# The opening attentions of a fused two-layer block: a third group's normalisation passes moved to ScalarE, a fourth group's statistics moved to other turns

## The chip, the core and the metric

The kernel runs on one core of a Trainium2 chip. The metric is device time in microseconds (us); the kernel before takes 888.03 us, the median of three runs (887.79 to 888.46). A difference of about 0.2% (1.8 us) is what a measurement of this kernel can tell from no change.

A core has engines that run their own instruction lists side by side and wait for one another by semaphores: TensorE (PE in the profile, its weight loads PEld), VectorE (DVE), ScalarE (ACT), GpSimd (POOL) and SyncE (SP, which here only issues DMA transfers).

## The reference, cut to what matters

The input x holds 64 sequences of 32 rows of 256 numbers. Six steps add to it in turn; each starts from a layer norm of x:

```
x = x + window cross attention(norm(x), ctx)   # 16 heads of 16, rotary
x = x + causal self attention(norm(x))         # 16 heads of 16, rotary
x = x + linear in fp8(norm(x))
x = x + cross attention over 257 keys(norm(x), ctx)
x = x + gated mixer(norm(x))
x = x + mixture of 8 experts, top 2, plus a shared one(norm(x))
```

The norm is `y = (x - mean) / sqrt(variance + 1e-5)` over the 256 numbers of a row. The change touches only the first step, and of it the norm of the third and fourth quarter of the rows.

## The kernel before, in words

The 2048 rows are four groups (g = 0 to 3) of 512 rows, a group being four tiles of 128 rows. `small_attentions` (L250) computes the first two steps as eight units of work, n = 0 to 7: layer one's groups 0 to 3, then layer two's. Before its loop it prepares units 0 and 1. The loop then goes over n, and in each n over four turns t = 0 to 3; a turn is written (n, t) here. In turn (n, t) the scores of tile t of unit n are computed, older tiles are carried on by one step each (turned, context, by_feature, project), and unit n+1 is prepared: `rotated` makes one half of its keys (t = 0, 1) or queries (t = 2, 3), `values` its values (even t), `spread_keys` spreads its keys by head.

Unit n+2 is prepared earlier still. `norm_steps` (L115) is a generator that gives its norm in four pieces: the statistics (four bn_stats on DVE), the aggregation with a start value for the inverse root (four bn_aggr and three small instructions on DVE) and three Newton steps on POOL (twelve small instructions on 128x4, called the root chain here), then the normalised rows y, two tiles at a time (one pass on DVE each, or, with `by_act`, one ACTIVATE on ACT with a scale and an offset; the offset takes two more small instructions on POOL). `prepare(count)` takes so many pieces. Which turn takes how many is written by hand in three tables of four numbers, `ahead` (before `rotated`), `behind` (after `by_feature`) and `at_end` (after the sums). `opened` transposes y on PE (eight transposes into two psT tiles) and ACT copies the two psT tiles to yT, from which the queries are made.

The order on each engine is as the code issues it, without a scheduler (`in_order`). All engines run their lists strictly in order, so an instruction that waits holds back what stands behind it. DMA issues stand in SP's list: the four swapped blocks of a rotation (far<-part), the values' way through memory (v_rows<-v, then vb<-v_rows in `blocks`), and loads of later weights and of x.

PSUM tiles of `rotated` (ps_qk), `values` (ps_v) and `opened` (psT) take three banks in turn (b0, b1, b2, in `pa`). So the second psT of turn (1, 0) needs the bank in which ps_qk of the same turn stands until ACT has read it (near<-ps_qk).

Of the kernel before, what the change touches and what calls it, by code (L numbers as in the profile page):

```python
# [20 lines left out]
NG, NT = 4, 4  # L21
# [44 lines left out]
def perceiver_kernel(ctx: ExitStack, tc: tile.TileContext, a: dict, out: bass.AP):  # L66
# [121 lines left out]
    def finish(pieces):  # L188

        while True:  # L190
            try:
                next(pieces)
            except StopIteration as end:
                return end.value

    def ring(pool, *tags):

        count = [0]

        def get(shape, name, dt=F32):  # L200
            tag = tags[count[0] % len(tags)]
            count[0] += 1
            return pool.tile(shape, dt, tag=tag, name=name, bufs=1)

        return get
# [13 lines left out]
    def transposed(y, bank, yT):  # L219

        for pair in range(y.shape[1] // 2):
            ps = bank([P, 2, 2 * P], "psT")
            for c in range(2):
                for i in range(2):
                    turn(
                        ps[:, c, i * P : (i + 1) * P],
                        y[:, 2 * pair + i, c * P : (c + 1) * P],
                        ident,
                    )
            scalar.copy(yT[:, :, pair * 2 * P : (pair + 1) * 2 * P], ps)  # L230
        return yT
# [18 lines left out]
    def small_attentions(layers, first_loads, decode, sides, load_layer1, layer1):  # L250
# [33 lines left out]
        def fetch(n):  # L284
            layer, g = order[n]
            if not layer["from_ctx"]:
                return None
            kvT = kvTs([P, 2, GT], "kvT")
            sync.dma_start(out=kvT, in_=a["ctx32T"][g])
            return kvT  # L290
# [6 lines left out]
        def group(n, kvT):  # L297

            layer, g = order[n]
            return dict(layer, n=n, g=g, kvT=kvT)  # L300

        def opened(it):
            yT = transposed(it["y"], pa, yTs([P, 2, GT], "yT"))
            it["yT"] = yT
            if not it["from_ctx"]:
                it["kvT"] = yT
# [78 lines left out]
        def blocks(it, half):  # L385
            vb = vbs[it["n"] % 2]
            it["vb"] = vb
            rows_h = v_rows[it["i"], it["g"]][half * D : (half + 1) * D].rearrange(
                "(b k) d -> k b d", k=S
            )  # L390
            for h in range(4):
                sync.dma_start(
                    out=vb[half][S * h : S * (h + 1), :, h].rearrange("k b g e -> k b (g e)"),
                    in_=rows_h[:, :, 64 * h : 64 * (h + 1)],
                )
# [108 lines left out]
        order = [(layer, g) for layer in layers for g in range(NG)]  # L504
# [15 lines left out]
        after = group(1, fetch(1))  # L520
# [6 lines left out]
        adds = [rotated(it, 1, c) for c in range(2)]  # L527
# [21 lines left out]
        now = it  # L549

        line = [None] * 5
        adds, early_y = [], None
        layer1_loads = load_layer1()
        for n in range(len(order) + 1):
            if n > 0:
                after = coming
            if after is not None:
                after["kb"] = [None, None]
            kvT = coming = None
            if n + 2 <= last:  # L560
                side = norm_steps(order[n + 2][1], apart=True)
            else:
                side = sides

            def prepare(count):
                y = None
                for _ in range(count if n + 2 <= last else 0):
                    try:
                        next(side)
                    except StopIteration as end:  # L570
                        y = end.value
                return y

            ahead, behind, at_end = (
                ((0, 1, 0, 1), (1, 0, 1, 0), (0, 0, 0, 0))
                if n
                else ((0, 0, 0, 0), (0, 0, 1, 0), (0, 1, 0, 2))
            )

            for t in range(NT):  # L580
                if (n, t) == (last + 1, 2):
                    shared_bank[0] = ring(psum, "b0", "b1")
                    late_bank.append(ring(psum, "b7", "b5"))
                if line[2]:
                    turned(line[2])
                kb_now = None
                if n <= last:
                    if t < 2:
                        kb_now = (now, 1, t)
                    elif after is not None:  # L590
                        kb_now = (after, 0, t - 2)
                due, adds = adds, []
                if t == 0 or n == 0:
                    for add in due:
                        add()
                    due = []
                    if n == last:
                        add_bias(n - 2, NT - 1)
                if kb_now:
                    spread_keys(*kb_now, 0)  # L600
                if line[4] and (n, t) != (last - 1, NT - 1):
                    project(line[4])
                if after is None:
                    next(layer1, None)
                else:
                    y = prepare(ahead[t])
                    adds.append(rotated(after, *((1, 0), (1, 1), (0, 0), (0, 1))[t]))
                    if (n, t) == (0, 0):
                        blocks(now, 0)
                    elif (n, t) == (0, 1):  # L610
                        opened(after)
                    elif (n, t) == (0, 3):
                        next(loads)
                    if (n, t) == (last - 1, NT - 1):
                        project(line[4])
                        sums(line[2])
                if line[3]:
                    by_feature(line[3])
                prepare(behind[t])
                if n + 2 > last:  # L620
                    next(side, None)
                    if n > last:
                        next(side, None)
                if n > 0 and (n, t) != (last - 1, NT - 1):
                    add_bias(n - 1, t)
                if n > 0 and (n, t) != (1, 0) and (t % 2 == 0 or n + 2 > last):
                    next(decode, None)
                for add in due:
                    add()
                if kb_now:  # L630
                    spread_keys(*kb_now, 1)
                if after is None:
                    next(layer1, None)
                elif t % 2 == 0:
                    values(after, t // 2)
                    if (n, t) == (0, 2):
                        blocks(now, 1)
                    elif (n, t) == (1, 0):
                        after["y"] = early_y
                        opened(after)  # L640
                elif t == 3:
                    for half in range(2 if n < last - 1 else 1):
                        blocks(after, half)
                    if n + 2 <= last:
                        coming = group(n + 2, kvT)
                        if n > 0:
                            coming["y"] = y
                            opened(coming)
                line[0] = scores(now, t) if n <= last else None
                if (n, t) == (last, NT - 1):  # L650
                    pair_pool.close()
                    later_psum.append(
                        attention.enter_context(tc.tile_pool(name="at_late", bufs=1, space=PSUM))
                    )
                if line[2]:
                    context(line[2])
                if (n, t) == (last - 1, NT - 1):
                    next(layer1)
                    blocks(after, 1)
                if line[1] and (n, t) != (last - 1, NT - 2):  # L660
                    sums(line[1])
                if last >= n > last - 2:
                    next(side, None)
                early_y = prepare(at_end[t])
                if t == (0 if n else 1) and n <= last - 2:
                    kvT = fetch(n + 2)
                elif n < 3 and (n, t) not in ((0, 0), (0, 2)):
                    next(loads, None)
                elif n >= last - 2:
                    next(layer1_loads, None)  # L670
                line = [None] + line[:-1]
            now = after
# [1548 lines left out]
```

## Time and profile before

| what | us |
|---|---|
| median of 3 runs | 888.03 |
| the profiled execution | 888.15 |
| its span, first to last instruction | 886.4 |
| what lies around the span | 1.75 |
| PE busy | 851.0 (96% of the span) |
| DVE, POOL, ACT busy | 576.1, 513.9, 438.5 |
| mean granted clock of TensorE | 0.992 |

Times within the kernel are us from the start of the span. A line of the timeline gives start, duration, engine, line (L107 and L119 are helpers that record nearly every operation), operation, output<-input with shapes, the number of instructions joined, and in square brackets how long the engine was idle before and what ended that idle time. The turns concerned begin with the transposes of probabilities on PE (ps_t<-cst,e): (1, 0) at 41.63, (1, 1) at 51.07, (1, 2) at 55.73, (1, 3) at 63.30, (2, 0) at 68.83 and (2, 1) at 75.22.

### The profile page before, as it was taken

What the parts mean: (1) busy time and instruction counts of PE and PEld (TensorE: products, weight loads), DVE (VectorE), ACT (ScalarE), POOL (GpSimd) and SP (SyncE); (2) the same over time, 40 slices, a digit from 0 to 9 for tenths busy, and PEclk for the clock granted to TensorE, in tenths of its full rate; (3) what the DMA queues carried; (4) which work ended last, traced back from release to release, by engine and by line L of the source; (5) the groups of instructions that cost most, each with busy time, mean ns of one, the idle gap of its engine ahead of it and who ended that gap; (6) DMA issues with size and microseconds to landing.
All of it is one profiled execution on the core that took longest, in us unless ns stands there. A gap on an engine that the chain in (4) does not pass through costs nothing. (4 is left out here: it accounts for less than half of the span.)

```text
span 886.4 us, 22890 instructions
## 1 busy us (share of the span) xinstructions
PE 851.0 (96%) x8729; PEld 586.9 (66%) x8729; DVE 576.1 (65%) x1692; ACT 438.5 (49%) x1135; POOL 513.9 (58%) x1004
## 2 busy tenths in 40 slices
PE   7989999999999999999999999999999999999995
PEld 3566666665466666666666665666667568888894
DVE  6888777896777576885778756866766861111116
ACT  2756667674654555565445645575652323222224
POOL 4677777785774657575575754685651254555430
PEclk9999999999999999999999999999999999999999
DMA  6564433553110111110111101120010046777768
GB/s 216 146 164 119 120 92 96 143 138 104 54 55 24 34 54 55 55 55 2 55 54 56 55 1 55 55 73 25 3 36 2 24 169 219 232 232 232 220 191 290
DMA packets 66926, 88.77 MB, mean 100 GB/s; under 512 B 32480, under 2 KB 50688, under 8 KB 64768
## 3 DMA queue, kind: packets, MB, share of 16 engines
q1 hardware_dynamic: 62592, 76.95, 28.9%
q0 software_dynamic: 3456, 9.44, 3.2%
q8 instruction: 69, 1.13, 0.5%
q10 hardware_dynamic: 768, 0.92, 0.4%
q14 instruction: 41, 0.34, 0.1%
HBM read 65.78 MB, written 13.11 MB: 89 GB/s over the span
## 5 line engine op out<-in xcount | busy, mean ns | idle before, releaser
L107 ACT ACTIVATE e<-e,xnm 128x257 f32<-128x257 f32 x256 | 127.2, 499 | 43.7 <-DVE xnm L107 40.4
L119 PE MATMUL ps_k<-ct,w_w_l1x 128*128 128x512 f32 x256 | 122.8, 602 | 1.1 <-ACT yT L107 0.5
L107 POOL TENSOR_SCALAR e<-e,xsm 128x256 f32<-128x256 f32 x256 | 123.4, 500 | 0.0
L107 DVE CUSTOM_DVE_ANT_0 e<-ps_s,mask 128x257 f32<-128x257 f32 x256 | 93.5, 421 | 43.3 <-PE ps_s L119 43.1
L119 PE MATMUL ps_v<-w_w_l1x,ct 128*128 128x256 f32 x512 | 121.1, 379 | 0.0
L122 PE MATMUL ps_t<-cst,e 128*128 128x128 f32 x640 | 101.7, 281 | 2.3 <-DVE eT L107 2.0
L119 PEld LDWEIGHTS ps_v<-w_w_l1x,ct 128*128 128x128 f32 x512 | 93.4, 190 | 10.8 <-ACT y L107 0.2
L107 DVE COPY eT<-ps_t 128x512 f32<-128x512 f32 x124 | 85.1, 686 | 23.4 <-PE ps_t L122 23.3
L107 ACT ACTIVATE kT<-ps_k,vec 128x512 f32<-128x512 f32 x64 | 44.0, 687 | 97.9 <-PE ps_k L119 96.4
L107 POOL TENSOR_TENSOR x<-x,rows 128x256 f32<-128x256 f32 x96 | 70.0, 747 | 28.2 <-DVE y L107 24.9
L107 ACT ACTIVATE hTr<-ps_h,w 128x256 f32<-128x256 f32 (+1 forms) x80 | 31.4, 450 | 110.3 <-issue 89.4
L122 PEld LDWEIGHTS ps_t<-cst,e 128*128 128x128 f32 x640 | 71.4, 140 | 20.1 <-DVE eT L107 4.8
L107 DVE TENSOR_TENSOR og<-ps_o,b 128x512 f32<-128x512 f32 (+1 forms) x20 | 12.8, 638 | 105.6 <-PE ps_o L119 105.6
L119 PEld LDWEIGHTS ps_k<-ct,w_w_l1x 128*128 128x128 f32 x256 | 44.6, 190 | 42.0 <-issue 34.1
L1964 POOL DMA_INDIRECT r_rows<-og,lv x36 | 35.5, 986 | 60.8 <-DVE og L107 55.9
L119 PE MATMUL ps_h<-ygT,w 128*128 128x256 f32 (+1 forms) x320 | 67.2, 364 | 0.0
L107 ACT COPY v<-ps_v 128x512 f32<-128x512 f32 x80 | 46.4, 581 | 41.1 <-PE ps_v L119 40.7
L107 POOL TENSOR_TENSOR last<-e,xsm 128x4 f32<-128x4 f32 x64 | 15.3, 238 | 88.6 <-DVE xsm L107 87.1
L119 PE MATMUL ps_o<-w,hTr 128*128 128x256 f32 x288 | 65.3, 379 | 0.0
L119 PEld LDWEIGHTS ps_h<-ygT,w 128*128 128x128 f32 x320 | 56.0, 194 | 6.4 <-issue 0.2
L119 PEld LDWEIGHTS ps_o<-w,hTr 128*128 128x128 f32 x288 | 54.4, 190 | 7.2
L107 ACT ACTIVATE kb<-kT,cst 128x256 f32<-128x256 f32 x96 | 45.4, 512 | 23.8 <-POOL kT L107 23.7
(225 smaller groups left out, 1671.4 us busy)
## 6 DMA issues: line engine op xcount, KB each, us to landing
ct<-in_ctxT SPq DMA_DIRECT2D x16, 1024.0 KB
w<-in_ew SPq DMA_DIRECT2D x20, 514.0 KB
w<-in_ew SPq DMA_DIRECT2D x20, 512.0 KB
far<-part SPq DMA_DIRECT2D x126, 64.0 KB
v_rows<-v SPq DMA_DIRECT2D x16, 256.0 KB
vb<-v_rows SPq DMA_DIRECT2D x64, 64.0 KB
r<-r_rows SPq DMA_DIRECT2D x8, 512.0 KB
b<-in_eb SPq DMA_DIRECT2D x20, 128.0 KB
```

Of the source, the lines that this page charges most:

```text
L107: ins = getattr(self.engine, name)(*args, **kw)
L119: return kept(nc.tensor.matmul(ps, **args))
L122: return kept(nc.tensor.transpose(ps, src, eye))
L1964: wrote = nc.gpsimd.indirect_dma_start(out=r_rows, out_offset=bass.IndirectOffsetOnAxis(ap=write_i[:, at : at + 1], axis=0), in_=o[:, i, : ...
```

## The change

Three things are done, all in units 0 and 1 of the loop.

- For n = 0, which prepares group 2, the norm is made with `by_act`: its four y passes go from DVE to ACT, and POOL gets two more small instructions (off). They stand at the end of turn (0, 3), where DVE's passes stood. The eight transposes and two copies of `opened` move from turn (1, 0) to turn (1, 1), behind that turn's rotation.
- For n = 1, which prepares group 3, the four pieces are taken at other places: the statistics at the end of (1, 0) instead of in its middle, aggregation and root chain at the end of (1, 1) instead of its beginning. The y passes stay on DVE and in their places, in the middle of (1, 2) and ahead of the rotation of (1, 3).
- `blocks(now, 1)`, four DMA issues of unit 0's values, moves in SP's list from turn (0, 2) to (0, 3), behind that turn's four far issues and ahead of the load of the last quarter of x.

From n = 2 on, the tables and calls are as they were.

```
-        adds, early_y = [], None
+        adds, rest = [], None
...
-                side = norm_steps(order[n + 2][1], apart=True)
+                side = norm_steps(order[n + 2][1], apart=True, by_act=(n == 0))
...
             ahead, behind, at_end = (
-                ((0, 1, 0, 1), (1, 0, 1, 0), (0, 0, 0, 0))
-                if n
-                else ((0, 0, 0, 0), (0, 0, 1, 0), (0, 1, 0, 2))
-            )
+                ((0, 0, 0, 0), (0, 0, 1, 0), (0, 1, 0, 1)),
+                ((0, 0, 0, 1), (0, 0, 1, 0), (1, 1, 0, 0)),
+                ((0, 1, 0, 1), (1, 0, 1, 0), (0, 0, 0, 0)),
+            )[min(n, 2)]
...
-                    elif (n, t) == (0, 1):
+                    elif t == 1 and n < 2:
                         opened(after)
                     elif (n, t) == (0, 3):
+                        blocks(now, 1)
                         next(loads)
...
                 elif t % 2 == 0:
                     values(after, t // 2)
-                    if (n, t) == (0, 2):
-                        blocks(now, 1)
-                    elif (n, t) == (1, 0):
-                        after["y"] = early_y
-                        opened(after)
...
-                early_y = prepare(at_end[t])
+                prepare(at_end[t])
+                if (n, t) == (0, NT - 1):
+                    coming["y"] = finish(side)
```

## The prediction, on record before the result was known

> **What bounds the kernel now.** I read the page first, then the windows of 10 us, PE's waits over the turns that change, then the timelines of PE, DVE and POOL there.
>
> ```profile
> PE 851.0 (96%) x8729; PEld 586.9 (66%) x8729; DVE 576.1 (65%) x1692; ACT 438.5 (49%) x1135; POOL 513.9 (58%) x1004
> ```
>
> PE is the bound: 96% busy, against 65% for the next engine. In the windows 60 to 70 and 70 to 80 it is busy 10.00 of 10.00 us. Of all its waits only 1.5 us are on DMA (kvT 1.2, ct 0.3); the others are on engines that follow PE. So I let a shift of PE at the start of turn (2, 0) pass through to the end one to one. PE's waits from 28 to 70 us:
>
> ```profile
> PE psT L122 <- ACT near L107: 1.6, 1, 1.6
> PE ps_p L119 <- ACT cT L107: 0.9, 1, 0.9
> ```
>
> Both lie in what changes. The first in the timeline of PE, in turn (1, 0):
>
> ```profile
> 46.98 0.60 PE L122 MATMUL psT<-cst,y 128*128 128x128 f32 x4
> 49.21 0.66 PE L122 MATMUL psT<-cst,y 128*128 128x128 f32 x4 [1.63 <-ACT near L107]
> 49.80 0.30 PE L119 MATMUL pair_bank<-mk,eye 64*32 64x256 bf16 x8
> ```
>
> The second psT needs a bank that ACT's near empties; near (48.47) waits for DVE's part (47.62), and part stands behind four y passes. DVE and POOL at that time:
>
> ```profile
> 43.94 3.42 DVE L107 TENSOR_SCALAR y<-x,mv,rn 128x256 f32<-128x256 f32 x4
> 47.29 0.41 DVE L107 TENSOR_TENSOR x<-ps_p,x 128x256 f32<-128x256 f32 x1
> 47.62 0.73 DVE L107 SCALAR_TENSOR_TENSOR part<-ps_qk,vec,cst 128x512 f32<-128x512 f32 x1
> 50.04 0.43 DVE L107 BATCH_NORM_STATS2 st<-x 128x6 f32<-128x256 f32 x1 [1.69 <-DMA x<-in_x]
> ```
> ```profile
> 43.86 1.27 POOL L107 TENSOR_TENSOR qT<-near,far 128x512 f32<-128x512 f32 x1
> 45.11 0.52 POOL L107 TENSOR_SCALAR kb<-kT,cst 128x256 f32<-128x256 f32 x1
> 45.59 1.30 POOL L107 TENSOR_TENSOR near<-near,cst 128x512 f32<-128x512 f32 x1
> 47.22 1.27 POOL L107 TENSOR_TENSOR qT<-near,far 128x512 f32<-128x512 f32 x1 [0.33 <-DMA far<-part]
> ```
>
> A y pass takes 0.40 us alone (shortest of the eight from 30 to 70 us) but these take 3.42 together: the first lasts 1.34 and ends at 45.28, 0.15 after POOL's qT; the third 1.35 and ends 0.15 after POOL's near. A y pass that begins beside a POOL instruction ends 0.15 after it. The second wait (0.92, before ps_p at 57.30) follows from DVE's chain below: aggregation ahead of part in (1, 1).
>
> The two idle stretches, 9.00 - 7.30 from 42 to 51 us and 7.60 - 6.68 from 55.7 to 63.3, are 2.62 us: the most that can be gained.
>
> **Turn (1, 0).** I walk the new order with the old durations. The y passes leave DVE (3.42); x and part run as soon as PE lets them: ps_qk ends at 45.19, part at about 45.97 instead of 48.35. ACT gets four passes; its y rows elsewhere (567 us) last 0.59 and follow each other at 0.50, so 3 x 0.50 + 0.59 = 2.09, from 44.46 (after off) to 46.55. Behind them stand eT, kb and near: 0.58 + 0.46, so near from 47.4 to 48.1, cT to 48.6: earlier than before (49.16 and 49.67), so ACT hides them, and without that cover they would cost up to 2.09.
>
> POOL pays. Its root chain is 12 instructions from 40.62 to 43.91 (0.27 each); off adds two, 0.5. Then qT 1.27, kb 0.48, near 1.27, qT 1.27: from 44.4 to 48.6. SP: the four far issues go ahead of four vb issues of 0.5, so far lands some 2 us earlier and the 0.33 wait goes; the x load stays at about 45.6, since eight issues precede it either way. vb lands 2.0 to 2.5 us after issue, before 48, and is wanted at 48.95. The scores (pair_bank<-kb,qT) need both qT, so they begin at 48.67: PE, free at 46.98, waits 1.7. **The wait for POOL takes the place of the wait for ACT.** But the eight transposes (0.91) are no longer before the scores. Turn (1, 1) begins at 49.54 instead of 51.07, and owes the 0.91: a lead of 0.62.
>
> **Turn (1, 1).** DVE: mx, sc, o, sm and reciprocal end at 51.7; four bn_stats 1.33 (x has landed at 50.0, so the 1.69 wait goes), x add at 53.0, part to 54.0. ACT: near 54.1, two yT copies, cT to 56.27 (before 57.25). PE has its transposes done at 53.7 and is ready for ps_p at 55.6; it waits 0.7 and starts at 56.3 instead of 57.30. Lead 0.98.
>
> **Turns (1, 2) and (1, 3): where I expect it to be lost.** Before:
>
> ```profile
> 54.97 0.17 DVE L107 TENSOR_SCALAR r<-half 128x4 int32<-128x4 int32 x1
> ...
> 60.19 0.75 DVE L107 SCALAR_TENSOR_TENSOR part<-ps_qk,vec,cst 128x512 f32<-128x512 f32 x1 [1.29 <-PE ps_qk L119]
> 60.85 1.26 DVE L107 TENSOR_SCALAR y<-x,mv,rn 128x256 f32<-128x256 f32 x2
> 62.04 0.62 DVE L107 CAST scratch<-raw 128x512 int32<-128x512 int8 x1
> 62.90 0.69 DVE L107 TENSOR_REDUCE mx<-pair_bank 128x16 f32<-128x512 f32 x1 [0.24 <-PE pair_bank L119]
> ```
> ```profile
> 58.31 0.20 POOL L107 TENSOR_TENSOR rn<-sq,rn 128x4 f32<-128x4 f32 x1
> 58.46 1.27 POOL L107 TENSOR_TENSOR near<-near,cst 128x512 f32<-128x512 f32 x1
> ```
>
> The chain ended at 58.51, 2.3 us before y wanted it. Now aggregation stands behind the sums: mx from 54.63, sc, o, sm, reciprocal (2.6), aggregation and start value (1.0): r at 58.25 instead of 55.14. POOL, by then through near and x add (56.85), has a kT add (1.27) in front of the chain, which needs its far; in the trace that far's last packet landed at 57.7. So the chain starts between 58.3 and 59.05 and ends between 61.6 and 62.35. DVE's two y passes wait for it, idle from 59.95, in front of the cast and of mx, though the scores are ready at 61.8. And POOL goes on at once with kb (0.48) and near (1.27): the passes end some 1.9 after the chain instead of 0.80. With the cast (0.62, less 0.1 overlap) mx starts at 64.0 to 64.8 instead of 62.90. o follows 1.74 later (mx 0.72, sc 0.61, o 0.41); PE wants it at 66.37 - 0.98 = 65.4. The second pair of y, behind sm, reciprocal and x, is done 3.7 after mx: 67.7 to 68.5. Its four transposes stood at 67.05; PE cannot pass them earlier. So turn (2, 0) comes 0.7 to 1.5 later than before. I take +1.4, near the late end, because the far landing of 57.7 is a row of the trace, and the early end needs it gone.
>
> On the blocking a rule of the Trainium skill bears (SBUF — State Buffer, "Who interferes with whom"): GpSimd and a VectorE instruction in a 2-port mode share a port pair, the later one blocks fully, and casts can be such instructions too. It speaks against leaving group 3's passes on DVE behind a late chain. By it the cast also waits, for POOL's x add, and the sum would be 0.3 us more; the trace's one cast (0.62 beside a POOL kb) does not settle that.
>
> **Sum.** 0 to 888.15 profiled: +1.4, 889.55; against the median, 888.03 + 1.4 = **889.4**.
>
> **Rivals.**
> - *Lead kept.* If y passes beside POOL ran at 0.40, or the root chain ended by 60, mx would be on time and the 0.5 to 1.0 lead stay: 887.0 to 887.5; if POOL were also 1.7 us quicker in (1, 0), up to the 2.62: 885.4. Against it: the rows 1.34 and 1.35, and r at 58.25, which hangs on five DVE instructions in a row.
> - *Second pair blocked too (slower).* If POOL is over 1 us later than I walk, the second pair at 67.6 meets its kT add or kb (done at 66.6 in my walk) and takes 1.3 more, less some of the first; from +0.4 beyond my sum it is slower by over 0.2%: 890.4, at most 891. For it: POOL has the longest queue here. Against it: POOL then idles for ACT's near.
> - *Only re-timed.* The waits trade places and nothing is won or lost by over 0.5: 888.0. For it: far lands early and the first y pair slips between two POOL instructions.
>
> **How the numbers follow.** Forecast 0.40, slower rival 0.34, lead kept 0.16 (of it 0.10 by over 1.8 us), re-timed 0.10. A measurement can tell about 0.2% (1.8 us) from no change. Slower by over that: 0.34; faster: 0.10; within: 0.40 + 0.10 + 0.06 = 0.56. The range takes in the first three cases but for their far ends: 887.0 to 891.0; the forecast's own is 888.6 to 889.8.
>
> **What would show it.** In the profile after: PE psT <- ACT near gone, and a pair_bank wait on POOL qT of 1 to 2 us near 48.7; ps_t of (1, 1) at 49.5; r near 58.3; DVE idle before y, ended by POOL rn; y x2 over 1.2 us; PE waiting for DVE's y near 68; (2, 0) later than 68.83. If (1, 2) shows no y wait, or if PE's shift at 70 us is not the shift at the end, I am wrong.

## The result, and the profile after

| kernel | median, us | runs | ratio to the kernel before | 95% interval |
|---|---|---|---|---|
| before, same chip | 887.87 | 12 | | |
| changed | 889.77 (888.99 to 893.62) | 12 | 1.0028 | 1.0017 to 1.0039 |
| before, a second comparison | 887.92 | 23 | | |
| changed, a second comparison | 888.99 (886.89 to 893.36) | 12 | 1.0014 | 1.0000 to 1.0029 |

The changed kernel is slower, by 1.9 us in the first comparison and by 1.1 us in the second. The forecast was +1.4. The first ratio lies beyond the 0.2% that counts as a difference, though its interval begins below it; the second does not. The forecast had given "within" 0.56 and "slower" 0.34.

The page of the changed kernel, its profiled execution of 888.99 us (span 887.2, mean clock 0.993), shows nothing: every engine is as busy as before.

```profile
PE 848.9 (96%) x8729; PEld 585.8 (66%) x8729; DVE 573.8 (65%) x1688; ACT 440.8 (50%) x1139; POOL 513.2 (58%) x1006
```

The turns do. These are their first transposes on PE (ps_t<-cst,e), in us from the start of the span; the last columns are counted from turn (1, 0) of the same execution, because the executions enter that turn up to 1.04 apart, for a reason that stands at the end.

| turn | before | changed | changed, second profile | before, from (1, 0) | changed | second |
|---|---|---|---|---|---|---|
| (1, 0) | 41.63 | 40.59 | 40.79 | 0 | 0 | 0 |
| (1, 1) | 51.07 | 48.61 | 48.85 | 9.44 | 8.02 | 8.06 |
| (1, 2) | 55.73 | 54.14 | 54.38 | 14.10 | 13.55 | 13.59 |
| (1, 3) | 63.30 | 61.41 | 61.64 | 21.67 | 20.82 | 20.85 |
| (2, 0) | 68.83 | 71.87 | 69.86 | 27.20 | 31.28 | 29.07 |
| (2, 1) | 75.22 | 78.39 | 76.24 | 33.59 | 37.80 | 35.45 |

So a lead of 0.82 to 0.85 us is built up to (1, 3), and in that one turn 4.93 and 2.69 us are lost. Behind (2, 0) the shift of the first profile against the kernel before stays: +3.04 there, +3.20 at 152 us, +2.85 at 466 us, +2.82 at 640 us. What ends PE's waits says why. The waits of PE from 27 to 73 us in the changed kernel (total, times, longest):

```profile
PE ps_c L122 <- DVE o L107: 2.4, 1, 2.4
PE pair_bank L119 <- POOL qT L107: 1.1, 1, 1.1
PE psT L122 <- DVE y L107: 0.7, 1, 0.7
```

These are three of its six rows. The wait for near is gone, the one for POOL's qT has its place, and two for DVE are new. The timeline of PE there:

```profile
67.03 0.44 PE L122 MATMUL ps_c<-cst,o 128*128 128x128 f32 x2 [2.38 <-DVE o L107]
67.31 0.60 PE L122 MATMUL psT<-cst,y 128*128 128x128 f32 x4
68.60 1.13 PE L122 MATMUL psT<-cst,y 128*128 128x128 f32 x4 [0.69 <-DVE y L107]
...
69.85 1.08 PE L119 MATMUL pair_bank<-kb,qT 64*32 64x128 f32 x32
```

The two brackets are the waits. The durations hold a third cost: the second four transposes take 1.13 where the first four take 0.60, and the scores take 1.08. The clock granted to TensorE is halved there. In the windows of the same kernel (length, then busy time and count for PE, PEld, DVE, ACT and POOL, then the granted clock, the DMA share and GB/s), the stretch behind the waits stands at 0.50, where the 4 us before it have 0.97:

```profile
69.00:72.20 3.20, 3.20 (x77) 2.28 (x78) 1.54 (x3) 2.67 (x7) 1.90 (x2) 0.50 0.26 60
```

Back along the chain, DVE and then POOL in the changed kernel:

```profile
57.04 0.17 DVE L107 TENSOR_SCALAR r<-half 128x4 int32<-128x4 int32 x1
...
62.63 1.83 DVE L107 TENSOR_SCALAR y<-x,mv,rn 128x256 f32<-128x256 f32 x2 [3.59 <-POOL rn L107]
64.38 0.94 DVE L107 CAST scratch<-raw 128x512 int32<-128x512 int8 x1
65.24 0.68 DVE L107 TENSOR_REDUCE mx<-pair_bank 128x16 f32<-128x512 f32 x1
```
```profile
58.08 1.27 POOL L107 TENSOR_TENSOR kT<-near,far 128x512 f32<-128x512 f32 x1 [2.17 <-DMA far<-part]
59.31 0.20 POOL L107 TENSOR_TENSOR sq<-r 128x4 f32<-128x4 f32 x1
...
62.39 0.20 POOL L107 TENSOR_TENSOR rn<-sq,rn 128x4 f32<-128x4 f32 x1
62.57 0.48 POOL L107 TENSOR_SCALAR kb<-kT,cst 128x256 f32<-128x256 f32 x1
63.01 1.30 POOL L107 TENSOR_TENSOR near<-near,cst 128x512 f32<-128x512 f32 x1
```

The start value r is ready at 57.21, but the root chain stands behind a kT add that waits 2.17 for its far, and ends at 62.59. DVE's y passes wait 3.59 for it. They end 0.14 after POOL's kb (at 63.19) and 0.15 after its near (at 64.46): two passes in 1.83, where one alone takes 0.40. The cast behind them ends 0.28 after POOL's next add, 0.94 instead of 0.41. mx, whose scores were done at 60.89, starts at 65.24, and o, which PE wants at 64.65, comes at 66.97.

### The profile page after: what moved, and what is told of

It is laid out like the page before. It is cut to its first block, busy times and chain, and to the rows that moved or that the text cites. A ratio compares the mean times of both kernels' runs of the same rounds, so it can differ in the third digit from the quotient of the medians.

```text
span 887.2 us, 22893 instructions
## 1 busy us (share of the span) xinstructions
PE 848.9 (96%) x8729; PEld 585.8 (66%) x8729; DVE 573.8 (65%) x1688; ACT 440.8 (50%) x1139; POOL 513.2 (58%) x1006
## 3 DMA queue, kind: packets, MB, share of 16 engines
q0 software_dynamic: 3456, 9.44, 3.2%
q8 instruction: 69, 1.13, 0.5%
```

## The experiments

The theory: the loss is one chain, the fourth group's late root chain, then y passes beside POOL, then mx and o, and the third group's move alone gains. The rivals put it on the third group (ACT's passes, POOL's two more instructions, the wait for qT) or on the transfers.

**The third group's part alone.** The changed kernel with the old tables from n = 1 on:

```
-                ((0, 0, 0, 1), (0, 0, 1, 0), (1, 1, 0, 0)),
                 ((0, 1, 0, 1), (1, 0, 1, 0), (0, 0, 0, 0)),
-            )[min(n, 2)]
+            )[min(n, 1)]
```

> The third group's part alone: its y passes on ACT and its transposes in (1, 1), and the fourth group's statistics in the turns they had before. Theory (the loss comes from the fourth group's late root chain, which holds DVE's y passes in (1, 2) and (1, 3)): the chain ends well before y wants it, no DVE idle time in front of y, the lead of 0.5 to 1.0 us that PE has in the changed kernel at (1, 2) is kept or partly eaten by bn_stats waiting for x in (1, 0); time between the kernel before and 1 us less. Rival (the third group's move itself costs: four ACTIVATEs of 0.59, two more POOL instructions, transposes in a fuller turn): about as slow as the changed kernel, 1.5 us or more over the kernel before.

Measured: 889.67 against 888.68, ratio 1.0010 [0.9993, 1.0027]; (1, 0) to (2, 0) 29.96, 2.76 more than before. That is a miss. The turn from (1, 0) to (1, 1) took 8.09, so the gain was there, but in the middle of (1, 0) the statistics of the fourth group now stand before x has landed. DVE's timeline in this kernel:

```profile
49.97 1.41 DVE L107 BATCH_NORM_STATS2 st<-x 128x6 f32<-128x256 f32 x4 [4.21 <-DMA x<-in_x]
```

The 4.21 us hold back the mx behind them (51.29) and all that follows on DVE, so that cT comes late and PE waits 2.49 us before ps_p at 58.18. A stretch at half clock follows that wait (58.15 to 61.57), and part of the 2.76 is that. So the third group's move does not stand by itself: without the slow passes DVE reaches the statistics before x has landed. With the statistics at the end of the turn, as in the change and in the kernels with the earlier chain below, this wait is not there.

**The fourth group's part alone.** The kernel before, with the new row of the table for n = 1:

```
-                ((0, 1, 0, 1), (1, 0, 1, 0), (0, 0, 0, 0))
-                if n
-                else ((0, 0, 0, 0), (0, 0, 1, 0), (0, 1, 0, 2))
-            )
+                ((0, 0, 0, 0), (0, 0, 1, 0), (0, 1, 0, 2)),
+                ((0, 0, 0, 1), (0, 0, 1, 0), (1, 1, 0, 0)),
+                ((0, 1, 0, 1), (1, 0, 1, 0), (0, 0, 0, 0)),
+            )[min(n, 2)]
```

> The fourth group's statistics alone in the changed turns, the third group as before. Theory: the loss is here; DVE idle before y in (1, 2) ended by POOL rn, PE waiting for DVE's o and y near 67 to 69; 1.5 to 3 us slower than the kernel before. Rival (third group's move costs): within 0.5 us of the kernel before.

Measured: 891.31, ratio 1.0020 [1.0002, 1.0037]; (1, 0) to (2, 0) 31.23, 4.03 more than before and as much as in the changed kernel (4.08). PE's waits in this kernel:

```profile
PE ps_c L122 <- DVE o L107: 2.1, 1, 2.1
PE psT L122 <- ACT near L107: 1.9, 1, 1.9
```

The loss is here, with the third group and the four DMA issues where they were. A stretch at half clock follows the wait here too (67.88 to 71.29), and the 4.03 contain it.

**The chain one piece earlier.** The changed kernel, with aggregation and root chain in the middle of turn (1, 1) instead of at its end: in front of the kT add.

```
-                ((0, 0, 0, 1), (0, 0, 1, 0), (1, 1, 0, 0)),
+                ((0, 0, 0, 1), (0, 1, 1, 0), (1, 0, 0, 0)),
```

> The changed kernel, but aggregation and root chain of the fourth group in the middle of (1, 1) instead of its end, so that POOL runs the chain ahead of the kT add that waits for far. Theory: the chain ends 3 us earlier (about 59.5), no y wait, PE keeps its lead of 0.5 to 1.0: 886.9 to 887.5 where the kernel before has 887.9. Rival (y passes blocked by POOL are the loss by themselves, however early the chain): still 1 us or more slower than the kernel before.

Measured: 886.87 against 888.68, ratio 0.9982 [0.9963, 1.0000]; (1, 0) to (2, 0) 26.72, 0.48 less than before. POOL and DVE in this kernel:

```profile
58.33 0.20 POOL L107 TENSOR_TENSOR rn<-sq,rn 128x4 f32<-128x4 f32 x1
```
```profile
59.02 1.68 DVE L107 TENSOR_SCALAR y<-x,mv,rn 128x256 f32<-128x256 f32 x2
60.62 0.41 DVE L107 CAST scratch<-raw 128x512 int32<-128x512 int8 x1
61.06 0.69 DVE L107 TENSOR_REDUCE mx<-pair_bank 128x16 f32<-128x512 f32 x1
```

The chain ends at 58.53, 4.06 earlier than in the changed kernel, and y waits for nothing. The passes are still slowed by POOL (1.68), but they are on time, and neither o nor y makes PE wait. Moving the chain by one piece takes the whole loss away and leaves a lead of 0.48 us at (2, 0).

**The same again, beside the changed kernel**, since the interval touched 1:

> The same kernel as the one with the fourth group's root chain one place earlier, beside the changed kernel on the same chip, because its interval touched 1. Theory (the lead that the third group's move makes is kept as soon as the fourth group's chain is on time): turn (2, 0) begins 26.7 us after turn (1, 0) (27.20 in the kernel before, 31.28 in the changed one), no wait of PE for o or y from 60 to 70 us, ratio to the kernel before 0.997 to 0.999, and 0.995 to 0.997 to the changed kernel. Rival (the lead is a chance of one execution): 27.2 or more, ratio 1.000 or above.

> The changed kernel itself, on the same chip as the kernel with the earlier chain. Theory: slower than the kernel before by 0.2 to 0.4%, PE waits of 2 to 2.8 us for o and of some 0.7 us for y near 67 us, and one stretch of 3.4 us at half clock right after them; if that stretch is missing in this execution, turn (2, 0) begins some 1.5 us less late. Rival (the stretch at half clock is a chance of one execution and no follower of the waits): the waits are there, the stretch is not, and the ratio stays as it was.

Measured: 886.44, ratio 0.9985 [0.9971, 0.9999], for the earlier chain, and 888.99, 1.0014 [1.0000, 1.0029], for the changed kernel: 2.55 us between the two medians. (1, 0) to (2, 0) took 26.73 with the earlier chain, 0.01 from the first time, and 29.07 in the changed kernel, 2.21 less than in its first profile. This second profile is the instructive one. In its timelines of POOL, DVE and PE, and in the window:

```profile
56.99 1.27 POOL L107 TENSOR_TENSOR kT<-near,far 128x512 f32<-128x512 f32 x1 [0.85 <-DMA far<-part]
```
```profile
57.08 1.21 DVE L107 TENSOR_SCALAR half<-ve 128x4 int32<-128x4 int32 x1
```
```profile
58.58 0.20 POOL L107 TENSOR_TENSOR sq<-r 128x4 f32<-128x4 f32 x1 [0.31 <-DVE r L107]
```
```profile
66.31 0.44 PE L122 MATMUL ps_c<-cst,o 128*128 128x128 f32 x2 [1.43 <-DVE o L107]
```
```profile
69.00:72.20 3.20, 3.20 (x67) 2.33 (x55) 2.68 (x6) 3.20 (x9) 2.63 (x3) 1.00 0.36 82
```

Here far lets the kT add start 1.09 earlier. The root chain behind it starts only 0.73 earlier (58.58), because after the kT add it still waits 0.31 for the start value r. The wait for o is 0.95 shorter, the one for y again 0.69, and the clock stays full. The expected 2 to 2.8 for o and 0.2 to 0.4% for the whole were missed (1.43 and 0.14%): this wait is not fixed, it hangs on a landing. Nor did the waits stand there unchanged without the half clock, as the rival had it: the shorter wait and the full clock came together. From (1, 3) to (2, 0) the two profiles took 10.46 and 8.22 us; of the 2.24, 0.95 is the wait and the remaining 1.29 the half clock.

**The chain on DVE.** The changed kernel, with the Newton steps of n = 1 on DVE, which has them behind the start value at once:

```
-                side = norm_steps(order[n + 2][1], apart=True, by_act=(n == 0))
+                side = norm_steps(order[n + 2][1], vector if n == 1 else None, apart=True, by_act=(n == 0))
```

> The changed kernel with the fourth group's root chain on DVE (nine small instructions) instead of POOL, in the same place of the order; DVE is idle then. Theory: the chain no longer stands behind POOL's kT add and its far, ends near 59.5, y is not late, and PE's lead is kept: 0.5 to 1.0 us under the kernel before. Rival (y passes blocked by POOL are enough by themselves): 1 us or more over the kernel before.

Measured: 887.12 against 887.50, ratio 0.9997 [0.9986, 1.0008]; (1, 0) to (2, 0) 27.17, 0.03 less than before, and no wait for o or y. The loss is gone, and the lead with it, so the expected 0.5 to 1.0 under the kernel before was missed. The chain ends at 60.44, and part, which stands behind it in DVE's list, comes at 60.69. The lead of 0.80 is still there at (1, 3) and goes in that turn, where PE now waits for cT:

```profile
62.78 1.13 PE L119 MATMUL ps_p<-w_w_l0x,cT 128*128 128x256 f32 x4 [0.42 <-ACT cT L107]
```

**A longer chain.** The changed kernel with five Newton steps instead of three for n = 1, which is eight more small instructions on POOL:

```
-        for _ in range(3):
+        for _ in range(rounds):
```

> The changed kernel with five Newton steps instead of three for the fourth group (eight more small POOL instructions, 2.2 us). Theory: everything from y on moves one to one: PE waits for o near 67 grow from 2.4 to about 4.6 us, turn (2, 0) 2.0 to 2.5 us later than in the changed kernel. Rival (the chain has slack and something else holds PE): under 0.5 us later.

Measured: 892.63, ratio 1.0061 [1.0044, 1.0078]. The chain ended 2.28 later (64.87 instead of 62.59), PE's wait for o grew from 2.38 to 4.52, and (2, 0), counted from (1, 0), came 2.33 later than in the changed kernel. The wait for o grows one to one with the chain: nothing else sets it. Behind it, two stretches at half clock follow instead of one (68.20 to 75.03), and the wait for y is gone.

**The y passes on ACT too.** The changed kernel with `by_act=(n < 2)`:

> The changed kernel with the fourth group's y passes on ACT too. Theory (y passes late by the chain and, on DVE, blocked by POOL): DVE is free of them, mx of (1, 2) starts with its scores, o is in time; ACT waits for the chain instead, and the second pair is ready near 67, so that PE waits about 1 to 2 us for it there: between the kernel before and the changed kernel. Rival (the chain's lateness does not matter, only the port): PE's lead is kept whole, 0.5 us or more under the kernel before.

Measured: 890.75, ratio 1.0029 [1.0015, 1.0043]. mx is on time (61.73) and the wait for o is gone, but (1, 0) to (2, 0) is 29.65, and the wait has moved. PE and ACT in this kernel:

```profile
68.11 0.33 PE L122 MATMUL psT<-cst,y 128*128 128x128 f32 x1 [2.06 <-ACT y L107]
```
```profile
63.45 1.09 ACT L107 ACTIVATE y<-x,off,rn 128x256 f32<-128x256 f32 x2 [2.19 <-POOL off L107]
...
67.47 1.07 ACT L107 ACTIVATE y<-x,off,rn 128x256 f32<-128x256 f32 x2
```

The first pair waits 2.19 for POOL's off, everything behind it in ACT's list moves back, and the second pair is late there as well; half clock follows (69.50 to 72.91). By the turns this kernel lies between the kernel before and the changed one, as expected; by the whole time it is no better than the changed kernel. POOL's late chain, not the engine of the passes, is what costs.

**PE kept busy through the wait**, to measure the half clock by itself. First with 20 matmuls more at the head of `by_feature` in turn (1, 3), into the bank of ps_c:

```
+            for _ in range(fill):
+                mm(ps_c[:, 0, :], lhsT=ident, rhs=ident, start=True, stop=True)
```

> The changed kernel with 20 more matmuls of 128x128 on PE in front of the transposes of (1, 3), where PE idles 2.4 us; what they write is overwritten. Theory of a clock share (the idle time is followed by 3.4 us at half clock, which costs up to 1.7 us more): no half clock near 69 us and 0.5 to 1.5 us faster than the changed kernel. Rival (the half clock comes as often in the kernel before, at another place, and costs nothing net): the same as the changed kernel, or slower by up to 0.5 us where the added matmuls outlast the wait.

Measured: 895.59, ratio 1.0066 [1.0043, 1.0089], a miss, and no answer: the fill began only at 67.91, after the same wait (2.34 <- DVE o), and took 6.20 us of its own. The half clock came all the same (68.76 to 72.17), with PE busy from the wait on. Then with ten into the next free bank, in front of `by_feature`:

```
+                    spare = pa([P, P], "ps_fill")
+                    pa.same_again()
+                    for _ in range(10):
+                        mm(spare, lhsT=ident, rhs=ident, start=True, stop=True)
```

> The changed kernel with 10 more matmuls of 128x128 (about 2.2 us on PE) ahead of the transposes of (1, 3), into a bank that is free by then, so that they fill PE's idle 2.4 us instead of standing behind the same wait. Theory (the idle time is followed by 3.4 us at half clock, which costs PE up to 1.7 us): no half clock between 60 and 75 us, and turn (2, 0) 1.0 to 1.7 us earlier than in the changed kernel, measured from the start of (1, 0). Rival (the clock follows something else): half clock near 68 us as before, turn (2, 0) where it was.

PE in this kernel:

```profile
65.43 2.40 PE L119 MATMUL ps_fill<-cst 128*128 128x128 f32 x20
```

The fill ran through the wait, ps_c began at 67.77 without one, the clock stayed at full speed from 60 to 75 us, and (1, 0) to (2, 0) took 29.81, 1.47 less than in the changed kernel. From ps_c on it is 3.54 to (2, 0) instead of 4.84: 1.30 of the 1.47 is the clock. The whole time does not show it: 891.16, ratio 1.0036 [1.0023, 1.0049] over only five runs, which overlaps the changed kernel's interval. The profiled execution of this kernel has other stretches at half clock (at 14.7, 608.7 and 680.3 us). What the fill saves over many executions stays open.

## Why the prediction was right in its mechanism, and short in its sizes

- *PE is the bound, and a shift at (2, 0) passes to the end.* Held through the middle: +3.04 at (2, 0), +2.82 at 640 us in the first profile, +1.03 and +0.73 in the second. The spans then differ by 0.8 and by 3.0, so the prediction's own sign of being wrong, a shift at 70 us that is not the shift at the end, is there in both profiles. Between 640 and 742 us the two shifts go from 2.82 to 0.86 and from 0.73 to 2.50, where each execution has its own stretches at half clock (before at 677.2 and 728.4; changed at 679.8; second profile at 676.8, twice as long, and at 731.4). Single executions do not settle it. Over the eleven comparisons of medians, the shift at (2, 0) counted from (1, 0) and the difference of the medians have the same sign each time and lie within 2.2 us of each other (4.08 and 1.9 for the change, -0.48 and -1.8 with the earlier chain, 7.87 and 6.9 with the fill of 20).
- *Turn (1, 0).* Held, but for one reading: the scores do not need both qT to begin. Four y passes on ACT took 2.08 (forecast 2.09) and are hidden. The wait for POOL's qT took the place of the one for near, 1.07 instead of 1.7, since half of the scores went first. (1, 0) to (1, 1): 8.02 (forecast 7.91).
- *Turn (1, 1).* Held: (1, 1) to (1, 2) took 5.53 (5.6), PE's wait for cT is 0.6 (0.7), and the lead at (1, 3) is 0.85 (0.98).
- *The chain behind the kT add.* The mechanism held, and its length of 3.28 (3.3). But it began at 59.31 and 58.58 in the two profiles. Counted from (1, 0), that is 18.72 and 17.79, where the forecast's 58.3 to 59.05 are 16.67 to 17.42. In the first profile the term that was mis-sized is the wait for far. It landed at 57.92, close to the forecast's 57.7, but this execution had entered (1, 0) 1.04 earlier and the landing did not come with it. The part that it carries was even done 3.40 earlier (44.95 instead of 48.35), yet its four issues stand in SP's list behind others, and these are their rows in the kernel before and in the changed one:

```profile
52.43 2.41 SPq L107 DMA_DIRECT2D far<-part  x4
```
```profile
52.38 2.41 SPq L107 DMA_DIRECT2D far<-part  x4
```

  An engine that runs ahead did not bring its transfer forward here. In the second profile far landed 16.05 after (1, 0), as forecast (16.1), and what the chain waited for last was r, which the kT add had held up (see the last section): a delay that the forecast did not have.
- *The y passes beside POOL.* They end 1.87 after the chain (forecast 1.9).
- *The cast.* The forecast gave it 0.62, as before, less 0.1 overlap. It took 0.94 beside POOL's x add, against 0.41 with the earlier chain, and mx started 0.78 after the passes' end instead of 0.52: 0.26 was missing. The Trainium skill (SBUF — State Buffer, "Who interferes with whom") had said that casts can be blocked by GpSimd too; the measurement agrees, and the sum by it (0.3 more) was nearer than the forecast's.
- *The second pair of y.* Forecast at 67.7 to 68.5; measured 68.77, and 68.05 in the second profile. It ran at full speed, 0.72 for two passes, so the rival that had it blocked too is not what made the loss larger.
- *What the forecast did not have at all:* the half clock, 1.3 us by the two profiles of the changed kernel and 1.3 by the fill. It came in one of the two profiles and not in the other; how often it comes over many executions, no run shows. The two medians differ by 0.8 us, with intervals that overlap, so that difference needs no cause.

The step that came out too small is "So turn (2, 0) comes 0.7 to 1.5 later than before": counted from (1, 0), it came 1.87 later without the half clock and 4.08 with it. That the forecast's +1.4 for the whole lies between the medians (+1.9 and +1.1) is in part luck: the terms were too small, and an execution has chances of its own of about that size, such as the 1.04 with which it enters turn (1, 0).

Beside this, the change carries a lead, as the rival "lead kept" said for a chain that ends by 60, and what it needs is small: the chain has to be in POOL's list before the add that waits for a transfer. Then the kernel is faster than the changed one by 2.55 us, and than the kernel before by 1.8 and 1.5 us in two comparisons (0.9982 and 0.9985), which is at the limit of what can be told; the second interval lies just below 1. The turns account for 0.48 of that, and where the rest comes from is open. How much of the lead is due to the four DMA issues that moved, no run separates from the third group's passes.

## What to carry to other kernels

Before a short chain is moved to "the end of the turn", look at what stands in front of it on its engine, and whether that waits for a transfer: in a strict list the chain inherits that wait, whatever its own inputs do. When work is moved forward, move only the engines' times forward, not the landings, until the DMA list has been walked too. And price a wait of the busiest engine at its length plus the slow clock that may follow it.

## What the runs showed of the hardware that was not expected

- **The clock falls after a wait far shorter than a stretch.** In each of twelve profiled executions (before, changed twice, nine others) the stretches at half clock lie on a grid of 3.413 us, which starts at another time in each execution: in before's they start at 15.0, 677.2 and 728.4 us, 194.0 and 15.0 steps apart. Adding up PE's idle time in each step of the grid up to 12 us from the end: all eleven steps with more than 1.84 us idle (1.96 to 3.41) are followed by half clock, in those from 1.58 to 1.84 it goes both ways, and below that it comes only behind a step already at half clock, or between 600 and 690 us behind steps without idle time, for a reason that stays open. The difference of 1.04 with which the executions enter turn (1, 0) is such a stretch too: before's has one at 15.0, behind a step with 1.96 idle, and the changed kernel's two profiles, with 1.43 and 1.32 there, have none. The five executions with a stretch near 14 to 15 us enter the turn at 41.32 to 41.63, the seven without it at 40.54 to 40.83. So in the first profile 1.68 of the wait for o and the 0.69 for y fall into one step (2.37 idle from 65.4 to 68.8), and another 1.3 us is paid; in the second the two waits are shorter and split over two steps (0.93 and 1.19), and nothing more is paid. The Trainium skill (TensorE: Matmul & The Clock Gate, "What's actually happening") has this window as free-running and 3413 ns long, which agrees; it has the clock fall after at least one idle window, where here about half a window was enough.
- **Small instructions of DVE are blocked as well.** In the second profile an instruction on 128x4 integers (half<-ve) took 1.21 instead of 0.17, from 57.08 to 58.29, beside POOL's kT add (56.99 to 58.26), and with the chain on DVE one scalar_tensor_tensor on 128x4 took 1.13 instead of 0.16 beside the same add. The first made POOL wait 0.31 for r.
- **It goes both ways.** In the kernel with the earlier chain, the kT add that began 0.14 after a y pass took 1.39 instead of 1.27.
